# Expert results re-laid by DMA and two transposes taken off TensorE, in a planned two-layer transformer kernel

## The chip, the cores and the metric

The kernel runs on one core of one Trainium2 chip. The metric is device time in microseconds (us): the median of several executions, each counted from start to end on the device. A profile is one further execution, recorded instruction by instruction.

## What is computed

The input x is 8 batches of 256 tokens with 128 channels, in fp32. Six residual blocks follow one another, cut here to what matters:

```python
x = x + 0.5 * soft_moe(layernorm(x))          # L0_ffn: 16 experts, 64 slots each
x = x + linear_attention(layernorm(x))        # L0_attn: 16 heads of 8
x = x + 0.5 * soft_moe(layernorm(x))
x = x + 0.5 * ternary_glu(layernorm(x))       # L1_ffn: 128 -> 512 -> 512 -> 512 -> 128
x = x + favor_attention(layernorm(x))         # L1_attn: FAVOR+, 32 features a head
x = x + 0.5 * ternary_glu(layernorm(x))

# soft_moe, per expert e (slots = dispatch-weighted sums of tokens, for every batch):
gate = gelu(slots @ Wg[e] + bg[e]); up = slots @ Wu[e] + bu[e]
eout = (gate * up) @ Wd[e] + bd[e]            # "second product": 256 -> 128
y = combine @ eout                            # over all 16 * 64 slots

# linear attention, last steps:            out = heads(q @ kv) / norm;  out @ Wproj.T + bproj
# FAVOR+: KV = phiK.T @ V, Ksum = sum(phiK);   (phiQ @ KV) / (phiQ @ Ksum);  @ Wo.T + bo
```

## The kernel before, in words

**Order.** The work is not issued in program order. Each piece is a step with the engines it may run on, an assumed cost in ns, the buffers it reads and writes, and a key. `Plan.place` (line 123) simulates five queues (PE, ACT, DVE, POOL, SP) with these costs and with the delays of `LAG`, picks at each point the step that can start first, and so fixes the order of every engine's instructions and the buffer slots. `SHIFTS` (line 16) moves the keys of parts of the program against each other; it changes the order only, not the work. Where the plan expects PE to idle for long, `idle` (line 1397) puts in products with the identity that nobody reads.

**Two groups.** Batches 0 to 3 and 4 to 7 are two groups (`group`, line 1366). The second has keys 45 us later, so that one group's TensorE-heavy stage can run beside the other group's stages of DVE, ACT and POOL. In each group: twice `dispatch` for four batches, then `experts` (16 experts for the four batches together, two 64-slot halves per 128 rows), then `combine` per batch; after the first of the two, `linear` per batch. Then `glu` for pairs of batches, `favor` per batch, and `glu` again.

**Dispatch** (594). The normalized y of a batch, 128 partitions with 2 x 128 values each, is needed in four copies with 32 tokens to each row block. `replicated` (573) writes y to DRAM with four DMAs of 32 partitions (`spill`, line 579) and reads it back four times with 32 partitions of 4 KB (`spread`, line 586). The gathering product (line 691) uses TensorE as four tiles of 32 rows.

**Experts** (749). For expert e, `fetch` loads the weights We (384 KB, line 764) and, at even e, the biases bd of two experts by a broadcast (line 767). There are four buffers for them. `front` makes the hidden layer with full-array products (line 787), Gelu on ACT (793) and the product of gate and up on DVE (798). `back` makes the second product for a pair of experts at once (line 818). Its stationary operand has 64 columns, one batch's slots, so TensorE works as two tiles of 128 rows x 64 columns, and the two experts' results come out in the two halves of the partitions, as `combine` (line 859) wants them. DVE adds the bias and writes into the slots buffer (830). `back` of a pair is called after the front of the expert that follows the pair.

**Transposes.** There are two ways. `flip` (line 375) is a TensorE transpose through the identity, followed by a copy out of PSUM (`evacuated`, 382 and 384). `squares_turned` (440) transposes 32x32 squares on DVE (446), writes the tile to DRAM with one DMA (449) and reads it back with four DMAs that put the squares in place (455). The second way is used for the normalized inputs of `linear`, `glu` and `favor` and for FAVOR+'s query features. The first is used, among others, in `project` (888), for linear attention's output ahead of the product with Wproj (907), and in `favor` for the 2 x 128 columns of sums (`turn_sums`).

**Products in fp32** show as two matmul instructions each in the trace; a transpose shows as one.

All DMAs are issued from SP's queue, in order. A DMA that has to wait holds back all that stand behind it.

Of the kernel before, what the change touches and what calls it, by code (L numbers as in the profile page):

```python
# [9 lines left out]
F32 = mybir.dt.float32  # L10
AF = mybir.ActivationFunctionType
ALU = mybir.AluOpType
AX = mybir.AxisListType
P = 128

SHIFTS = (
    -2751, -1692, -1691, -12195, -784, -1588, -17523, -441, -1660, -895, -929, -659, -543, -591,
    -517, -633, -219, -357, -610, -370, -144, -340, -138, -261, -103, -124, -149, -112, -87,
    328, -365, -173, -179, -134, 14, 40, -32, 136, -182, -43, -162, -672, 13, -20, 26, 13, -393,
    -13, -49, 76, 108, 25, -337, -106, -98, -405, -124, -14, 106, -15, -91, -232, -26, -141, 72,  # L20
    179, -149, -60, -56, -94, -291, -910, -397, 168, -109, -149, -2, -601, -150, 12, -21, -762,
    -20, -100, 231, -63, -522, -971, -639, -490, -1134, 34, -143, -240, -1126, 30, 98, 272,
    -229, -245, 48, 535, -647, -666, -418, 7, 144, -282, -73, 220, 168, 36, -1118, -353, -720,
    -886, -200, -34, 24, 100, 11, -24, 70, 30, -50, -121, 47, 25, 9, -51, 143, -939, -125, -300,
    -662, -491, -371, -203, -437, -21, -285, -479, -125, 412, 243, 49, 284, 369, 566, -147,
    -339, 157, 267, -173, -269, 162, -518, -492, 53, 116, -414, -523, -222, -451, -400, -304,
    -82, 145, -77, -134, -36, -467, -865, -141, -372, -407, -524, -134, 12, 58, -154, 246, 41,
    -111, 22, 62, -756, -131, 38, -435, -1331, -683, -948, -2046, -2339, -2000, -3450, -2514,
    -3516, -3317, -2307, -1684,
)  # L30


# [184 lines left out]
def macaron_kernel(ctx: ExitStack, tc: tile.TileContext, i: dict, out: bass.AP):  # L217
# [10 lines left out]
    nc = tc.nc  # L228
    B, N, D = out.shape
    TT = N // P  # L230
# [126 lines left out]
    def ps_(*shape):  # L357
        return Buf("ps", (P, *shape))
# [4 lines left out]
    def dve(n, extra=0):  # L363
        return 58 + 1.07 * n + extra
# [4 lines left out]
    def flips(n):  # L369
        return 109.5 * n  # L370
# [3 lines left out]
    def flip(po, src):  # L374
        nc.tensor.transpose(po, src, ident)  # L375
# [64 lines left out]
    def squares_turned(z, n, cells, dst, out):  # L440


        flat = lambda: z()
        there = dram.tile([P, n // 32, 32], F32, tag=f"t{len(turns)}", name=f"t{len(turns)}")
        turns.append(there)
        step({"DVE": 58 + 1.07 * n}, lambda _: nc.vector.transpose(z(), z()), cells, cells)

        def spill(_):
            nc.sync.dma_start(there.rearrange("p k j -> p (k j)"), z())


        def place(_):
            squares = there.rearrange("(a i) (t f) j -> f i t a j", a=4, f=4)
            for f in range(4):
                nc.sync.dma_start(
                    dst()[32 * f : 32 * f + 32].rearrange("p (t a j) -> p t a j", a=4, j=32),
                    squares[f],
                )

        step({"SP": 475}, spill, cells, [there.name], lag=1.5 * n)  # L460
        step({"SP": 2000}, place, [there.name], out, lag=2.5 * n)

    turns = []

# [103 lines left out]


    dram = ctx.enter_context(tc.tile_pool(name="dram", bufs=1, space=bass.MemoryType.DRAM))  # L570
    spilled = [dram.tile([32, N // 32, D], F32, tag=f"y{b}", name=f"y{b}") for b in range(B)]

    def replicated(y, b):

        yr = Buf("k4", (P, N // 32, D))

        def spill(_):
            for k in range(4):
                nc.sync.dma_start(
                    spilled[b].rearrange("i (t k) d -> i k t d", k=4)[:, k],  # L580
                    y.ap[32 * k : 32 * k + 32],
                )

        def spread(_):
            for a in range(4):
                nc.sync.dma_start(yr.ap[32 * a : 32 * a + 32], spilled[b])

        step({"SP": 2500}, spill, [(y, t) for t in range(TT)], [("y", b)], lag=-1500)
        step({"SP": 1765}, spread, [("y", b)], [yr], lag=900)
        return yr  # L590


# [1 line left out]
    def dispatch(b, sl):  # L594
# [92 lines left out]
        def gathered(_):  # L687
            for c in range(N // 32):
                for a, po in enumerate(pos):
                    rows = slice(32 * a, 32 * a + 32)  # L690
                    mm(  # L691
                        po.ap, yr.ap[rows, c, :], ex.ap[rows, :, 32 * c : 32 * c + 32],
                        start=(c == 0), stop=(c == N // 32 - 1), tile_position=(32 * a, 0),
                    )

# [52 lines left out]

    def experts(sl):
        def whole(j):  # L750
            return [(sl, j, q) for q in range(BG)]

        filled = [(sl, "in", q, a) for q in range(BG) for a in range(4)]

        def eo():
            return sl.ap.rearrange("p j k b s -> p j (k b s)").rearrange(
                "p j (b n) -> p j b n", n=2 * S1
            )

        def fetch(e):  # L760
            we = Buf("we", (P, 6 * P + D))

            def run(_):
                nc.sync.dma_start(we.ap[:, 0 : 6 * P], i["We"][e])
                if e % 2 == 0:
                    for k in range(2):
                        nc.sync.dma_start(
                            we.ap[S * k : S * k + S, 6 * P :],
                            i["bd"][e + k].partition_broadcast(S),
                        )  # L770

            step(
                {"SP": 475 if e % 2 else 1400}, run, [(sl, "in", BG - 2, 0)], [we],
                lag=1900 if e % 2 else 1000,
            )
            return we

        def front(e, we):
# [28 lines left out]
                step({"DVE": dve(256, 59)}, up, [pe, ga], [(ht, c)])  # L807
            return ht

        def back(j, wes, hts):  # L810

            po = ps_(BG, P)

            def down(_):
                for q in range(BG):
                    for c in range(2):
                        for k in range(2):
                            mm(  # L818
                                po.ap[S * k : S * k + S, q, :], hts[k].ap[:, c, ts(q, S)],
                                wes[k].ap[:, ts(4 + c, P)], start=(c == 0), stop=(c == 1),  # L820
                                tile_position=(0, S * k),
                            )

            step(
                {"PE": 1880}, down,
                [*wes, *((ht, c) for ht in hts for c in range(2))], [po],
            )

            def biased(_):
                nc.vector.tensor_tensor(  # L830
                    eo()[:, j, :, 0:D], po.ap,
                    wes[0].ap[:, 6 * P :].unsqueeze(1).to_broadcast([P, BG, D]), ALU.add,
                )

            step({"DVE": dve(512)}, biased, [wes[0], po], whole(j))

            def twos(_):
                nc.gpsimd.memset(eo()[:, j, :, D : D + 1], 2.0)

            step({"POOL": 65}, twos, [], whole(j))  # L840

        got = []
        for e in range(E):
            plan.part()
            we = fetch(e)
            got.append((we, front(e, we)))
            if e % 2 == 0 and e:
                back(e // 2 - 1, *zip(*got[e - 2 : e]))
        back(NJ - 1, *zip(*got[E - 2 :]))
        return eo  # L850

    def combine(b, comb, sl, eo):
# [3 lines left out]
        for t in range(TT):  # L856
            def gather(_, t=t):
                for j in range(NJ):
                    mm(  # L859
                        po.ap[:, t, 0 : D + 1], comb.ap[:, j, ts(t, P)], eo()[:, j, q, 0 : D + 1],  # L860
                        start=(j == 0), stop=(j == NJ - 1),
                    )

            step(
                {"PE": mms(*[D + 1] * NJ)}, gather,
                [(comb, u) for u in range(4)] + [(sl, j, q) for j in range(NJ)], [(po, t)],
            )
        rc = Buf("sm", (P, TT))

# [17 lines left out]

    def project(b, oh, w):

        pt = ps_(TT, P)  # L890
        ot = Buf("k1", (P, N))

        def turn(_):
            for t in range(TT):
                flip(pt.ap[:, t, :], oh.ap[:, t, :])

        step({"PE": flips(TT)}, turn, [oh], [pt], takes=[ot])
        evacuated(lambda: ot.ap, lambda: pt.ap.rearrange("p t c -> p (t c)"), [pt], [ot], N)
        projected_onto(b, ot, w)

    def projected_onto(b, ot, w):
# [291 lines left out]
    def favor(b):  # L1193
# [103 lines left out]
            [(phi, 0, c) for c in range(4)],  # L1297
            lambda: qk.ap.rearrange("p a b n -> p (a b n)"), [(qk, t) for t in range(TT)],
        )
        pk, pkt = ps_(2, P), ps_(2, P)  # L1300
        kvm = Buf("k1", (P, 2, P))

        def sums(_):
# [13 lines left out]
                m4of.unsqueeze(1).unsqueeze(3).to_broadcast([P, 2, 4, M]), ALU.mult,  # L1317
            )

        def turn_sums(_):  # L1320
            for m in range(2):
                flip(pkt.ap[:, m, :], kvm.ap[:, m, :])

        step(
            {"PE": 1020}, sums, [*((phi, 1, c) for c in range(4)), v1], [pk], takes=[kv, kvm]
        )
        step({"DVE": 340}, blocks, [pk], [kvm])
        step({"PE": flips(2)}, turn_sums, [kvm], [pkt])
        evacuated(
            lambda: kv.ap, lambda: pkt.ap.rearrange("p a (c n) -> p a c n", c=4), [pkt], [kv], N  # L1330
        )


# [148 lines left out]
```

## Time and profile before

| | before |
|---|---|
| median of 3 runs | 740.42 us (740.34 to 740.69) |
| the profiled execution | 743.85 us |
| its span, first to last instruction | 742.1 us |
| granted TensorE clock | 0.998 |
| TensorE (PE) busy | 728.8 us, 98% |
| DVE / ACT / POOL busy | 517.2 / 410.7 / 306.1 us |
| packets of the kernel's DMA queue, share of 16 engines | 30.6% |

The profiled execution has 1.75 us outside its span and is 3.4 us longer than the median. PE is busy when any matmul is in flight; matmuls overlap, so the "mean ns of one" of a matmul is longer than the distance between two of them. PEld is the load of the stationary operand. SPq is SP's queue, which issues the DMAs. In the rows of groups, the columns are line, engine, operation, written<-read tiles, shape and count, then busy us and mean ns of one, then idle time ahead.

### The profile page before, as it was taken

The numbers are of one execution on the slowest core, as the hardware profiler recorded it, in microseconds if no ns is written. First come the engines' busy times: TensorE is split into PE (matmuls) and PEld (weight loads), VectorE is DVE, ScalarE is ACT, GpSimd is POOL, SyncE is SP. The second block draws the span as 40 slices with busy tenths as digits, with TensorE's granted clock in tenths as the row PEclk, the third lists the DMA queues.
The fourth block names the chain that finished last, engine by engine and source line by source line (L and its number), as shares of the span: only waits on it lengthen the run. The fifth ranks groups of instructions, "written<-read, shape, count | busy, mean of one in ns | idle before, by whom it ended". The sixth has DMA issues, their size and how long they took to land.

```text
span 742.1 us, 15296 instructions
## 1 busy us (share of the span) xinstructions
PE 728.8 (98%) x5814; PEld 609.5 (82%) x5814; DVE 517.2 (70%) x1103; ACT 410.7 (55%) x774; POOL 306.1 (41%) x419
## 2 busy tenths in 40 slices
PE   8999999998999999999999999999999999999998
PEld 7878888997889988889878879788687677878787
DVE  6999965577868798975564274455998978855442
ACT  4889967257665577884553240433555664363331
POOL 7989446133427752459910022000745545211000
PEclk9999999999999999999999999999999999999999
DMA  5553432333330526333631210200344244120100
GB/s 143 150 140 118 139 93 94 109 81 97 126 114 2 146 83 197 99 94 119 171 99 52 85 29 1 57 0 15 78 114 95 42 118 81 32 60 14 42 1 29
DMA packets 102105, 62.34 MB, mean 84 GB/s; under 512 B 73104, under 2 KB 88848, under 8 KB 102032
## 3 DMA queue, kind: packets, MB, share of 16 engines
q1 hardware_dynamic: 102032, 61.36, 30.6%
q8 instruction: 46, 0.75, 0.4%
q14 instruction: 27, 0.22, 0.1%
HBM read 49.80 MB, written 11.53 MB: 83 GB/s over the span
## 4 chain that ended last, share of the span: by engine, by line
PE 87%; DVE 5%; DMA 3%; SPq 2%; issue 1%; POOL 1%; ACT 1%; POOLq 0%
PE ps L1077 27%; PE ps L787 14%; PE ps L818 8%; PE ps L859 8%; PE ps L691 6%; PE ps L615 4%; PE ps L1177 4%; PE ps L1147 4%; PE ps L1150 4%; PE ps L375 2%; DMA we<-in_We 1%; PE ps L1256 1%; DVE k L632 1%; PE ps L1307 1%; PE ps L1341 1%; PE ps L907 1%
## 5 line engine op out<-in xcount | busy, mean ns | idle before, releaser
L787 PE MATMUL ps<-slots,we 128*128 128x256 f32 x512 | 121.8, 384 | 4.0 <-DMA we<-in_We 2.3
L787 PEld LDWEIGHTS ps<-slots,we 128*128 128x128 f32 x512 | 94.7, 191 | 20.1 <-issue 5.2
L1077 PE MATMUL ps<-comb,slots 128*128 128x256 f32 x448 | 103.1, 381 | 0.0
L1077 PE MATMUL ps<-comb,comb 128*128 128x256 f32 x448 | 102.5, 381 | 0.0
L1077 PEld LDWEIGHTS ps<-comb,slots 128*128 128x128 f32 x448 | 83.6, 190 | 15.4 <-issue 3.9
L1077 PEld LDWEIGHTS ps<-comb,comb 128*128 128x128 f32 x448 | 83.6, 190 | 13.6 <-issue 2.5
L737 POOL TENSOR_TENSOR comb<-comb,k 128x1024 f32<-128x1024 f32 x32 | 75.1, 2369 | 33.5 <-DVE k L384 14.0
L793 ACT ACTIVATE k<-ps,small 128x256 f32<-128x256 f32 x128 | 56.5, 475 | 48.4 <-PE ps L787 46.1
L382 ACT COPY k<-ps 128x512 f32<-128x512 f32 (+2 forms) x55 | 28.5, 519 | 93.8 <-PE ps L1077 83.1
L670 POOL TENSOR_TENSOR comb<-comb,sm 128x1024 f32<-128x1024 f32 x32 | 60.9, 1911 | 41.4 <-DVE sm L665 41.4
L798 DVE SCALAR_TENSOR_TENSOR k<-ps,small,k 128x256 f32<-128x256 f32 x128 | 57.2, 475 | 29.2 <-ACT k L793 28.5
L412 POOL TENSOR_SCALAR sm<-sm 128x2 f32<-128x2 f32 x52 | 10.0, 193 | 153.1 <-DVE sm L406 140.1
L657 ACT ACTIVATE comb<-comb,sm 128x256 f32<-128x256 f32 x128 | 63.3, 497 | 13.7 <-PE ps L691 7.4
L1091 DVE TENSOR_TENSOR comb<-ps,k 128x512 f32<-128x512 f32 x48 | 32.9, 687 | 49.0 <-PE ps L1077 25.5
L818 PEld LDWEIGHTS ps<-we,k 128*64 128x64 f32 x1024 | 55.3, 137 | 9.2 <-issue 4.7
L615 PE MATMUL ps<-k,seT 128*128 128x256 f32 x256 | 61.7, 383 | 0.8 <-DVE k L495 0.5
L818 PE MATMUL ps<-we,k 128*64 128x128 f32 x1024 | 62.2, 275 | 0.0
L691 PE MATMUL ps<-comb,k 32*128 32x256 f32 x1024 | 59.9, 380 | 0.1
L859 PEld LDWEIGHTS ps<-slots,comb 128*128 128x128 f32 x512 | 58.4, 192 | 1.5 <-issue 1.3
L859 PE MATMUL ps<-slots,comb 128*128 128x129 f32 x512 | 59.6, 276 | 0.0
L1099 ACT ACTIVATE comb<-comb 128x512 f32<-128x512 f32 x48 | 30.0, 629 | 51.0 <-DVE comb L1091 50.8
L691 PEld LDWEIGHTS ps<-comb,k 32*128 32x128 f32 x1024 | 51.4, 185 | 5.6 <-issue 1.4
(144 smaller groups left out, 1303.7 us busy)
## 6 DMA issues: line engine op xcount, KB each, us to landing
we<-in_We SPq DMA_DIRECT2D x64, 384.0 KB, 3.8
k<-y SPq DMA_DIRECT2D x64, 128.0 KB, 2.9
t<-comb SPq DMA_DIRECT2D x8, 512.0 KB, 2.8
k<-t SPq DMA_DIRECT2D x32, 128.0 KB, 3.5
y<-k SPq DMA_DIRECT2D x64, 32.0 KB, 1.9
we<-in_bd SPq DMA_DIRECT2D x64, 32.0 KB, 3.6
t<-k SPq DMA_DIRECT2D x16, 128.0 KB, 1.7
k<-t SPq DMA_DIRECT2D x64, 32.0 KB, 2.3
```

The lines of the kernel that those rows point to most:

```text
L615: mm(pl.ap[:, j, :], seT[:, 2 * u + j].rearrange("p k s -> p (k s)"), yt.ap, start=True, stop=True,)
L657: nc.scalar.activation(ex.ap[:, 4 * h + j, :], comb.ap[:, 4 * h + j, :], AF.Exp, bias=mx.ap[:, j : j + 1], accum_out=mx.ap[:, 4 + j : 5 + j],)
L670: nc.gpsimd.tensor_tensor(ex.ap[:, part], ex.ap[:, part], mx.ap[:, 8:12].unsqueeze(2).to_broadcast([P, 4, N]), ALU.mult,)
L691: mm(po.ap, yr.ap[rows, c, :], ex.ap[rows, :, 32 * c : 32 * c + 32], start=(c == 0), stop=(c == N // 32 - 1), tile_position=(32 * a, 0),)
L737: nc.gpsimd.tensor_tensor(raw, raw, mb.ap.unsqueeze(1).to_broadcast([P, 4, N]), ALU.subtract)
L787: mm(pe.ap[:, m, :], we.ap[:, ts(2 * m + c, P)], sl.ap[:, j, k, :, 0:S], start=True, stop=True,)
L793: nc.scalar.activation(ga.ap, pe.ap[:, 0, :], AF.Gelu, bias=bg[:, e, c : c + 1])
L798: nc.vector.scalar_tensor_tensor(ht.ap[:, c, :], pe.ap[:, 1, :], bu[:, e, c : c + 1], ga.ap, ALU.add, ALU.mult,)
L818: mm(po.ap[S * k : S * k + S, q, :], hts[k].ap[:, c, ts(q, S)], wes[k].ap[:, ts(4 + c, P)], start=(c == 0), stop=(c == 1), tile_position=( ...
L859: mm(po.ap[:, t, 0 : D + 1], comb.ap[:, j, ts(t, P)], eo()[:, j, q, 0 : D + 1], start=(j == 0), stop=(j == NJ - 1),)
L1077: mm(bank.ap[:, o], w(k)[:, c, ts(o, P)], rhs().rearrange("p (c n) -> p c n", c=2)[:, c, :], start=(start and o + c == 0), stop=(stop and ...
L1091: nc.vector.tensor_tensor(C(i, k)(), bank.ap.rearrange("p o n -> p (o n)"), other(), ALU.add)
```

## The change

Four things change in the work.

- `replicated`: y goes to DRAM with one DMA of 128 partitions. The four reads fetch 32 x 4 pieces of 1 KB each in place of 32 of 4 KB, and the gathering product picks its columns by another index.
- `experts`: the second product is made for one expert at a time, right after the next expert's front, with full-array products: the stationary operand holds 128 slots, of two batches. The result is added to the bias in a buffer `moved` of 128 x 2 x 128, and two DMAs move its halves into the slots buffer. The bias comes with We from the host, already broadcast (448 KB a fetch), and the DMAs for bd are gone.
- `project`: the transpose of linear attention's output goes by `squares_turned`.
- `favor`: the transpose of the sums goes by `squares_turned`.

The planner's assumed costs of the DMA steps are others, and all of `SHIFTS` is replaced. The diff, with the numbers of `SHIFTS` and the host's lines cut:

```diff
 SHIFTS = (
-    -2751, -1692, -1691, -12195, -784, -1588, -17523, -441, -1660, -895, -929, -659, -543, -591,
...
+    -2645, -927, -925, -41, -149, -109, -109, -110, -145, -159, -38, -195, -225, 8, 143, -82,
...
 )
...
-        step({"SP": 475}, spill, cells, [there.name], lag=1.5 * n)
-        step({"SP": 2000}, place, [there.name], out, lag=2.5 * n)
+        step({"SP": 335}, spill, cells, [there.name], lag=1.1 * n - 850)
+        step({"SP": 2400 + 0.7 * n}, place, [there.name], out, lag=1.2 * n - 300)
...
-    spilled = [dram.tile([32, N // 32, D], F32, tag=f"y{b}", name=f"y{b}") for b in range(B)]
+    spilled = [dram.tile([P, N], F32, tag=f"y{b}", name=f"y{b}") for b in range(B)]
...
         def spill(_):
-            for k in range(4):
+            nc.sync.dma_start(spilled[b], y.ap.rearrange("p t d -> p (t d)"))
+
+        def spread(_):
+            blocks = spilled[b].rearrange("(k i) n -> i k n", k=4)
+            for a in range(4):
                 nc.sync.dma_start(
-                    spilled[b].rearrange("i (t k) d -> i k t d", k=4)[:, k],
-                    y.ap[32 * k : 32 * k + 32],
-                )
-
-        def spread(_):
-            for a in range(4):
-                nc.sync.dma_start(yr.ap[32 * a : 32 * a + 32], spilled[b])
-
-        step({"SP": 2500}, spill, [(y, t) for t in range(TT)], [("y", b)], lag=-1500)
-        step({"SP": 1765}, spread, [("y", b)], [yr], lag=900)
+                    yr.ap[32 * a : 32 * a + 32].rearrange("i (k t) d -> i k (t d)", t=TT), blocks
+                )
+
+        step({"SP": 335}, spill, [(y, t) for t in range(TT)], [("y", b)], lag=-500)
+        step({"SP": 1830}, spread, [("y", b)], [yr], lag=900)
         return yr
...
-                        po.ap, yr.ap[rows, c, :], ex.ap[rows, :, 32 * c : 32 * c + 32],
+                        po.ap, yr.ap[rows, TT * (c % 4) + c // 4, :], ex.ap[rows, :, 32 * c : 32 * c + 32],
...
             def run(_):
-                nc.sync.dma_start(we.ap[:, 0 : 6 * P], i["We"][e])
-                if e % 2 == 0:
-                    for k in range(2):
-                        nc.sync.dma_start(
-                            we.ap[S * k : S * k + S, 6 * P :],
-                            i["bd"][e + k].partition_broadcast(S),
-                        )
...
+                nc.sync.dma_start(we.ap, i["We"][e])
+
+            step({"SP": 475}, run, [(sl, "in", BG - 2, 0)], [we], lag=1500)
             return we
...
-        def back(j, wes, hts):
-
-            po = ps_(BG, P)
+        def back(e, we, ht):
+
+
+            j, k = e // 2, e % 2
+            po = ps_(NB, P)
+            moved = Buf("k1", (P, NB, P))
 
             def down(_):
-                for q in range(BG):
+                for r in range(NB):
                     for c in range(2):
-                        for k in range(2):
-                            mm(
-                                po.ap[S * k : S * k + S, q, :], hts[k].ap[:, c, ts(q, S)],
-                                wes[k].ap[:, ts(4 + c, P)], start=(c == 0), stop=(c == 1),
-                                tile_position=(0, S * k),
-                            )
...
+                        mm(
+                            po.ap[:, r, :], ht.ap[:, c, ts(r, P)], we.ap[:, ts(4 + c, P)],
+                            start=(c == 0), stop=(c == 1),
+                        )
 
             def biased(_):
                 nc.vector.tensor_tensor(
-                    eo()[:, j, :, 0:D], po.ap,
-                    wes[0].ap[:, 6 * P :].unsqueeze(1).to_broadcast([P, BG, D]), ALU.add,
-                )
...
+                    moved.ap, po.ap, we.ap[:, 6 * P :].unsqueeze(1).to_broadcast([P, NB, P]),
+                    ALU.add,
+                )
+
+            def place(_):
+                for h in range(2):
+                    nc.sync.dma_start(
+                        eo()[S * k : S * k + S, j, h::2, 0:D], moved.ap[S * h : S * h + S]
+                    )
...
+            step({"PE": mms(*[P] * 4)}, down, [we, (ht, 0), (ht, 1)], [po], takes=[moved])
+            step({"DVE": dve(256)}, biased, [we, po], [moved])
+            step({"SP": 1340}, place, [moved], cells, lag=-300)
...
-            if e % 2 == 0 and e:
-                back(e // 2 - 1, *zip(*got[e - 2 : e]))
-        back(NJ - 1, *zip(*got[E - 2 :]))
+            if e:
+                back(e - 1, *got[e - 1])
+        back(E - 1, *got[E - 1])
         return eo
...
     def project(b, oh, w):
 
-        pt = ps_(TT, P)
         ot = Buf("k1", (P, N))
-
-        def turn(_):
-            for t in range(TT):
-                flip(pt.ap[:, t, :], oh.ap[:, t, :])
-
-        step({"PE": flips(TT)}, turn, [oh], [pt], takes=[ot])
-        evacuated(lambda: ot.ap, lambda: pt.ap.rearrange("p t c -> p (t c)"), [pt], [ot], N)
+        squares_turned(
+            lambda: oh.ap.rearrange("p t d -> p (t d)"), N, [oh], lambda: ot.ap, [ot]
+        )
         projected_onto(b, ot, w)
...
-        step({"PE": flips(2)}, turn_sums, [kvm], [pkt])
-        evacuated(
-            lambda: kv.ap, lambda: pkt.ap.rearrange("p a (c n) -> p a c n", c=4), [pkt], [kv], N
+        squares_turned(
+            lambda: kvm.ap.rearrange("p a n -> p (a n)"), N, [kvm],
+            lambda: kv.ap.rearrange("p a c n -> p (a c n)"), [kv],
         )
```

## The prediction, made before the result was known

> **What bounds the kernel now.** I read the page first: the engines' busy shares, and the chain that ended last.
>
> ```profile
> PE 728.8 (98%) x5814; PEld 609.5 (82%) x5814; DVE 517.2 (70%) x1103; ACT 410.7 (55%) x774; POOL 306.1 (41%) x419
> PE 87%; DVE 5%; DMA 3%; SPq 2%; issue 1%; POOL 1%; ACT 1%; POOLq 0%
> ```
>
> TensorE is the bound from end to end: a change gains what it takes out of PE, and loses what it makes PE wait. Next, how much PE waits (columns: us in total, times, longest us):
>
> ```profile
> PE ps L787 <- DMA we<-in_We: 2.3, 2, 2.2
> PE ps L1399 <- POOL ident masks.py:199: 1.6, 1, 1.6
> PE ps L787 <- ACT comb L657: 1.2, 1, 1.2
> PE ps L375 <- DVE k L708: 1.1, 1, 1.1
> ```
>
> All such waits together are 8.9 us, so a better order alone can't win more than that. The costliest groups give the work that the change touches:
>
> ```profile
> L818 PE MATMUL ps<-we,k 128*64 128x128 f32 x1024 | 62.2, 275 | 0.0
> L859 PE MATMUL ps<-slots,comb 128*128 128x129 f32 x512 | 59.6, 276 | 0.0
> L375 PE MATMUL ps<-ident,k 128*128 128x128 f32 x112 | 23.5, 288 | 3.2 <-DVE k L708 1.1 <-POOL k L420 0.7 <-DVE k L1000 0.5
> ```
>
> A busy PE isn't a PE at its peak, so I went to PE's timeline, where the distance between the starts of two rows is what a block really takes. Around the last second product:
>
> ```profile
> 438.72 3.62 PE L1077 MATMUL ps<-comb,slots 128*128 128x256 f32 x16
> 442.26 1.97 PE L818 MATMUL ps<-we,k 128*64 128x128 f32 x32
> 444.16 1.99 PE L1077 MATMUL ps<-comb,slots 128*128 128x256 f32 x8
> 445.99 1.28 PE L859 MATMUL ps<-slots,comb 128*128 128x129 f32 x10
> ```
>
> and around a block of two pairs:
>
> ```profile
> 221.04 3.71 PE L818 MATMUL ps<-we,k 128*64 128x128 f32 x64
> 224.68 0.43 PE L375 MATMUL ps<-ident,sm 128*128 128x128 f32 x2
> ```
>
> One pair takes 442.26 to 444.16, 1.90 us, two take 3.64, so a pair in full flow takes 1.74 (54.5 ns an instruction) and 0.16 is paid on entry. The neighbours pay too. Full-array 256-column instructions follow each other every 216 ns (eight in 1.73 us in the chain). The x16 ahead takes 3.54 where 16 x 0.216 is 3.46 (+0.08), the x8 behind takes 1.83 (+0.10). So one excursion into 128x64 tiles costs 0.16 + 0.08 + 0.10 = 0.34 us, with no wait shown. Between full-array blocks nothing is paid: the eight L787 just ahead (436.99 to 438.72) take the plain 1.73.
>
> **The second product.** Removed: 1024 instructions at 54.5 ns, 55.8 us. Added: 64 experts x 8 = 512 full-array instructions. The nearest row is L859's (128 stationary columns, 129 moving): the chain has 32 of them in 3.57 us, 111.6 ns each, so 57.1 us. In full flow that is 1.3 us worse. The switches: the timeline has 28 blocks of L818. Twenty stand between full-array blocks and save 0.34 each, 6.8. Eight stand beside a block in 32-row or 32-column tiles, which pays a switch anyway; there I take the entry alone, 0.16, so 1.3. Sum: 1.3 - 6.8 - 1.3 = **-6.8 us** on PE. The Trainium skill, TensorEngine Tiling (Array Packing), section "Theoretical Speedup", speaks against the change: a stationary side of up to 64 columns gains up to 2x from packing. By that rule alone, with the 128 columns filled by two batches' slots, the two forms tie; by the rows' full-flow rates the change loses 1.3. The same page's "Key Properties" says that a change of tiling mode drains the array, with no price. The rows put 0.34 us on it, 28 times, and I take the rows.
>
> Beside PE: 64 DVE adds of 128x256 from PSUM (413 ns, L911) for 32 of 128x512 (688 ns), +4.4 us on an engine at 70%. SP issues 128 more DMAs of 32 KB (0.59 us each by y<-k, 75.5 us) and 64 fewer bd (0.59 us, -37.8). The add waits for `down` as before. The two DMAs wait for the add, and behind them in SP's queue stand We fetches and the other group's spills: about 0.41 + 1.2 us for each. That hits little, since a fetch has to wait for the buffer that the same `down` frees. SP's waits show it (L764 behind L818: 112.4 us in 18 waits). The pairwise `back` frees two of four buffers at once, one front (1.73 us) before the next weights are wanted; 3.8 us to landing doesn't fit, and PE's 2.3 us wait on We is the remnant. Freed one by one, the lead is two experts, 2 x (1.73 + 0.90) = 5.3 us, against about 6 (1.6 of hold, 4.4 for 448 KB in proportion): closer, not ample. Ends 0 and -2.3; I take **-1**.
>
> What is late next is `combine`: at the end of each of four expert blocks the last result comes after 0.41 + 1.2 + about 1.9 us to landing, 3.5 in place of 0.69. Cover at the last block was one L1077 product (444.16 to 445.99), and more of these stand ready; the earlier blocks have the other group's work. Ends 0 and 4 x 2.8 = 11.2; the nearest row has cover, so **+1**.
>
> **The two turns.** Removed: 16 times two transposes at 109 ns, 32 x 0.109 = **-3.5 us** on PE, and 16 copies out of PSUM (0.37 to 0.41 us). Added: 16 DVE transposes (0.44, L446), and on SP 16 x (0.33 + 4 x 0.61) = 44 us:
>
> ```profile
> k<-y SPq DMA_DIRECT2D x64, 128.0 KB, 2.9
> y<-k SPq DMA_DIRECT2D x64, 32.0 KB, 1.9
> ...
> t<-k SPq DMA_DIRECT2D x16, 128.0 KB, 1.7
> k<-t SPq DMA_DIRECT2D x64, 32.0 KB, 2.3
> ```
>
> The delay grows: 0.44 + 0.33 + 1.7 + 2.45 + 2.3 = 7.2 us (the same turn of linear's input ran from 141.32 to 150.43, 9.1 us), for 1.09 from flip to L907 (167.34 to 168.43). So +6.1 to +8.0 us a turn. FAVOR+'s eight lie among L1077 products of another pair: nothing. Linear's eight lie between `combine` and the next `dispatch`; only the last batch of each group delays the experts, so two exposures, up to 2 x 6.1 = 12.2 us. Between 160 and 170 us PE alternates linear's pieces with L787 of the other group: cover exists, though small waits at 175.8, 269.5, 272.1 and 291.6 us say that it isn't ample. Ends 0 and 12.2; **+2**.
>
> **One spill of y.** SP saves 4 x 0.59 - 0.33 = 2.0 us on each of 16 dispatches (the 0.33 is t<-k, the same 128 x 1 KB). The reads get four times the pieces: by 0.42 (k<-y) and 0.61 (k<-t, smaller pieces yet) I take +0.1 us each, 0.4 a dispatch. This is behind PE except in the first 56 us, where the chain, in order of time, runs through eight such issues:
>
> ```profile
> 43.72 0.55 SPq L579
> ...
> 48.11 0.04 issue
> 48.16 2.57 DMA y<-k
> 50.73 0.01 issue
> 50.74 1.93 DVE k L708
> ```
>
> Two spills in place of eight DMAs take 0.66 for 4.4 us there. But DVE is busy 49.8 of those 56 us and will be the next bound. Ends 0 and -3.8; **-1.5**, a little over PE's 1.1 us wait behind L708.
>
> **Order.** The new assumed costs are nearer to the rows (a placement 2579 ns for 4 x 0.61; it was 2000). Nothing of its own: 0, within the 8.9 us of waits either way.
>
> **Sum:** -6.8 - 1 + 1 - 3.5 + 2 - 1.5 = -9.8 us. The profiled execution's span goes from 742.1 to 732.3 (743.85 to about 734 with what lies around it). The median lies 3.4 us below that execution, so I take the same difference from it: 740.42 - 9.8 = 730.6.
>
> **Rivals.** (a) All added waits find cover, and the start and the We waits give their full ends: -6.8 - 3.5 - 3.8 - 2.3 = -16.4, 724.0. For it: PE's long list of ready products after 380 us. Against: DVE in the first 56 us. (b) PE loses its 10.3 us, but hops and turns lay half of it bare (+5.5) and nothing else comes: 735.6. For it: the small waits at 160 to 292 us. (c) Slower: SP's queue at the layer change. Each group's four linear turns add 4 x 2.77 = 11 us of issues where four input turns and four spreads already stand, and the hops of the other group's experts wait among them; a placement that waits for its spill holds the We fetches, L787 starves, and the cover goes with it. It decides once over 5.2 us is bare at each of the two changes; at 7 us each, 740.4 - 10.3 + 14 = 744. For it: SP's in-order queue, 112 us of fetch waits. Against: the spills give back 2.0 us per dispatch at that very place. (d) The change doesn't do what it says: the 0.16 us on entry belongs to stationary operands that are loaded late and not to the tiles, so 64 single blocks pay it too. Then the second product costs +1.3 - 8.1 + 64 x 0.16 = +3.4, the turns give back 3.5, the rest is +0.5: 740.8. Against: the neighbours' 0.08 and 0.10, and full-array blocks side by side that pay nothing.
>
> **How the numbers follow.** Chances: the sum 0.56 (730.6, from 726 to 735), (a) 0.12, (b) 0.17, (c) 0.10, (d) 0.05. A measurement can tell 0.2% (1.5 us) from no change. Faster: the sum, (a) and (b), 0.85; same: (d), 0.05; slower: (c), 0.10. The range takes in (a) and (b) and stops short of (d) and (c): 723.5 to 739.
>
> **What would show it.** Right: the second product in 512 full-array instructions at 112 ns, its neighbours at plain rates, PE busy down by about 10 us, transposes x80 for x112, PE's wait list still under 10 us. Wrong: PE waits on slots<-k or k<-t DMAs, L787 behind We for over 3 us, or idle products (L1399's) in the middle of the run.

## The result: 1.1% slower, and the profile after

| | before | changed |
|---|---|---|
| median (range) | 740.51 us (740.34 to 740.69) | 748.88 us (746.72 to 751.30) |
| ratio to before, 95% interval | | 1.0114 (1.0078 to 1.0150) |
| profiled execution / its span | 743.85 / 742.1 us | 747.5 / 745.8 us |
| PE waits, sum of the list | 8.9 us | 20.9 us |
| span less these waits | 733.2 us | 724.9 us |
| time of SP's DMA issues, summed over the trace | 249 us in 457 | 315 us in 553 |

The forecast was 730.6. The two profiled executions differ by 3.7 us and the medians by 8.4: what lies between a profiled execution and the median (3.4 us before) did not carry over. The changed kernel's executions spread over 4.6 us, these four of before over 0.35; but 55 later ones of the kernel before spread over 5.0 (738.3 to 743.3), so the narrow range says little.

A part of those 3.4 us can be seen in the profile of before. Behind its longest wait on We (2.2 us, over at 182.3) the granted TensorE clock is 0.50 from 183.0 to 186.4 us. A windows view of the stretch (length, busy us and instructions of PE, PEld, DVE, ACT, POOL, then clock, DMA share, GB/s) reads

```profile
180.00:190.00 10.00, 7.83 (x36) 6.73 (x36) 6.22 (x17) 4.82 (x10) 2.70 (x3) 0.83 0.47 117
```

so some 1.7 us of clock are lost there (10 x 0.17, an estimate); with the wait that is 3.9 us. The execution was a rare one: of 92 later executions of the kernel before, 90 show a clock of 0.999 or 1.000 over the whole span, and the two at 0.998, like this one, took 742.9 and 743.3 us. The changed kernel's profiled execution shows 1.000; its slowest, of 751.3 us, 0.995.

Busy shares, and the chain that ended last, from the changed kernel's page:

```profile
PE 721.0 (97%) x5262; PEld 609.0 (82%) x5262; DVE 518.3 (69%) x1133; ACT 421.1 (56%) x784; POOL 312.1 (42%) x421
PE 72%; DMA 13%; SPq 7%; DVE 4%; issue 2%; POOL 1%; ACT 1%; DVEq 0%; POOLq 0%; ACTq 0%
```

PE is busy 7.8 us less, as it was meant to be, though some of that is the clock of before. But the chain is no longer PE's: DMA and SP's queue hold 20% of it, for 5% before. What PE waits for in the changed kernel (total, times, longest, us; L897 is the product after linear attention's turn, L777 the experts' first, L918 linear's first, L1195 and L1327 FAVOR+'s):

```profile
PE ps L897 <- DMA k<-t: 7.9, 5, 3.0
PE ps L777 <- DMA we<-in_We: 4.4, 7, 1.4
PE ps L918 <- DMA k<-t: 2.2, 2, 1.9
PE ps L1385 <- POOL ident masks.py:199: 1.6, 1, 1.6
PE ps L1195 <- DMA k<-t: 1.5, 2, 1.3
PE ps L1327 <- DMA kv<-t: 1.5, 2, 1.2
```

The longest, in the chain of the changed kernel (start us, us, what):

```profile
201.99 4.11 DMA t<-k
206.11 0.02 issue
206.12 0.61 SPq L454
...
208.04 0.04 issue
208.09 2.26 DMA k<-t
210.35 0.14 issue
210.48 0.68 PE ps L897 x4
```

A turn's spill is in flight for 4.11 us, where the median is 2.0. It was issued right behind two hops and a We load, as SP's timeline shows:

```profile
200.01 1.25 SPq L823 DMA_DIRECT2D slots<-k  x2
201.36 0.54 SPq L763 DMA_DIRECT2D we<-in_We  x1
201.99 0.39 SPq L448 DMA_DIRECT2D t<-k  x1
206.12 2.58 SPq L454 DMA_DIRECT2D k<-t  x4
```

PE works in order: the L777 products behind L897 wait with it, and show no wait of their own.

```profile
210.48 0.68 PE L897 MATMUL ps<-WprojT,k 128*128 128x128 f32 x4 [2.99 <-DMA k<-t]
211.00 1.03 PE L777 MATMUL ps<-slots,we 128*128 128x256 f32 x4
```

Most of the loss is in one stage: of the 12.0 us by which the listed waits grew, 9.7 lie between 160 and 310 us. The windows view of that stage, of the kernel before:

```profile
160.00:310.00 150.00, 146.15 (x1235) 128.03 (x1235) 123.93 (x289) 103.46 (x219) 73.37 (x105) 0.99 0.36 102
```

and of the changed kernel:

```profile
160.00:310.00 150.00, 137.16 (x1084) 122.61 (x1084) 115.64 (x281) 91.94 (x198) 63.51 (x95) 1.00 0.51 142
```

PE is busy 9.0 us less in these 150 us, and the DMA engines' share rises from 0.36 to 0.51. The issues and landings of the changed kernel:

```profile
we<-in_We SPq DMA_DIRECT2D x64, 448.0 KB, 4.2
k<-y SPq DMA_DIRECT2D x64, 128.0 KB, 2.8
slots<-k SPq DMA_DIRECT2D x128, 64.0 KB, 2.5
t<-k SPq DMA_DIRECT2D x32, 128.0 KB, 2.0
```

A hop (slots<-k: one of the two DMAs that move an expert's result into the slots buffer) is 64 KB. The prediction had 32.

### The profile page after: what moved, and what is told of

It is laid out like the page before. It is cut to its first block, busy times and chain, and to the rows that moved or that the text cites. A ratio compares the mean times of both kernels' runs of the same rounds, so it can differ in the third digit from the quotient of the medians.

```text
span 745.8 us, 14551 instructions
## 1 busy us (share of the span) xinstructions
PE 721.0 (97%) x5262; PEld 609.0 (82%) x5262; DVE 518.3 (69%) x1133; ACT 421.1 (56%) x784; POOL 312.1 (42%) x421
## 4 chain that ended last, share of the span: by engine, by line
PE 72%; DMA 13%; SPq 7%; DVE 4%; issue 2%; POOL 1%; ACT 1%; DVEq 0%; POOLq 0%; ACTq 0%
PE ps L1067 21%; PE ps L777 11%; PE ps L854 7%; PE ps L690 6%; PE ps L810 6%; PE ps L614 5%; SPq L454 5%; DMA we<-in_We 4%; DMA t<-k 3%; PE ps L1137 3%; PE ps L1140 3%; DMA k<-t 3%; PE ps L1167 3%; PE ps L374 1%; PE ps L1327 1%
## 5 line engine op out<-in xcount | busy, mean ns | idle before, releaser
L777 PE MATMUL ps<-slots,we 128*128 128x256 f32 x512 | 121.7, 382 | 4.6 <-DMA we<-in_We 4.4
L777 PEld LDWEIGHTS ps<-slots,we 128*128 128x128 f32 x512 | 93.1, 190 | 20.8 <-issue 6.1
L381 ACT COPY k<-ps 128x512 f32<-128x512 f32 (+2 forms) x50 | 25.4, 507 | 72.7 <-PE ps L1067 58.8
L810 PEld LDWEIGHTS ps<-we,k 128*128 128x128 f32 x512 | 63.9, 192 | 2.7 <-issue 0.6
L810 PE MATMUL ps<-we,k 128*128 128x128 f32 x512 | 65.7, 275 | 0.0
L411 POOL TENSOR_SCALAR sm<-sm 128x2 f32<-128x2 f32 x52 | 10.3, 199 | 109.1 <-DVE sm L405 106.4
```

The lines of the kernel that those rows point to most:

```text
L777: mm(pe.ap[:, m, :], we.ap[:, ts(2 * m + c, P)], sl.ap[:, j, k, :, 0:S], start=True, stop=True,)
L810: mm(po.ap[:, r, :], ht.ap[:, c, ts(r, P)], we.ap[:, ts(4 + c, P)], start=(c == 0), stop=(c == 1),)
```

## The experiments

Theories: **W**, the turns' own delay; **S**, the hops crowd SP's queue (S1) and the DMA engines (S2), and what else comes by DMA is late; **O**, the new order is poor by itself. In e1 to e7 the changed kernel's order is kept instruction by instruction. The interval of the changed kernel is 2.7 us to either side, so a difference from it is known to about 3 us.

**e1 and e2: nobody waits for the turns.**

```diff
-                mm(po.ap[:, t, :], ot.ap[:, ts(t, P)], w, start=True, stop=True)
+                mm(po.ap[:, t, :], ident if free else ot.ap[:, ts(t, P)], w, start=True, stop=True)
```

and in e2 FAVOR+'s `kv.ap[:, m, c, :]` becomes `ones32` as well.

> The changed kernel in its own order, but linear attention's output product reads the identity in place of the turned array: the turn's DVE transpose and its five DMAs a batch are still issued, and TensorE waits for none of them (the output leaves attention's result out). Theory W (TensorE's in-order queue reaches that product before the turned array has landed, 7.9 us of waits in the changed kernel's profile): 739 to 741 us, 8 to 10 under the changed kernel. Theory S (the experts' hops crowd SP's queue and the DMA engines and make all that comes by DMA late): at most 3 us faster, 746 or more, with the waits moving to the expert weights. Theory O (the new order is poor by itself): 746 or more.

> As the run before it, and FAVOR+'s product over the sums reads a constant of ones as well, so neither of the two new turns is waited for (the sums are left out of the result). W: another 1.5 to 2.5 us under the run before it, about 737 to 739, since the changed profile shows 1.9 us of TensorE waits on that turn. S and O: no change against the run before it beyond 1 us.

e1: 742.44 us, ratio 1.0042 (1.0027 to 1.0056), 6.4 under the changed kernel and between what W and S had asked for. e2: 742.75, 1.0038 (1.0026 to 1.0049), no better. In e2, PE's wait list has more on We (4.4 us in the changed kernel):

```profile
PE ps L777 <- DMA we<-in_We: 7.3, 8, 1.4
```

With nothing to wait for at either turn the kernel is still 0.4%, some 3 us, slower than before. The turn is where most of the loss shows, not all that makes it: W is half right at best.

**e3: no hops.** The add writes into the slots buffer, and `place` issues nothing.

```diff
-                    moved.ap, po.ap, we.ap[:, 6 * P :].unsqueeze(1).to_broadcast([P, NB, P]),
+                    eo()[:, j, 2 * k : 2 * k + 2, 0:D], po.ap,
+                    we.ap[:, 6 * P :].unsqueeze(1).to_broadcast([P, NB, P]),
```

> The changed kernel in its own order, but the DVE add writes its result straight into the slots buffer, in the wrong rows, and the 128 DMAs of the hops are gone (expert results are mixed between slots). W: linear's turn is still waited for, with somewhat shorter landings: 743 to 747. S: SP loses 76 us of issues and all waits behind them; spills and weights land in time, 738 to 741. O: 746 or more.

730.80 us, 0.9874 (0.9858 to 0.9890): 18.1 us under the changed kernel, more than any theory asked for. PE's longest waits in e3:

```profile
PE ps L894 <- DMA k<-t: 2.1, 3, 1.1
PE ps L1382 <- POOL ident masks.py:199: 1.6, 1, 1.6
PE ps L915 <- DMA k<-t: 0.5, 1, 0.5
```

and e3's window from 160 to 310 us:

```profile
160.00:310.00 150.00, 147.35 (x1155) 133.48 (x1155) 124.83 (x302) 102.08 (x218) 70.89 (x101) 1.00 0.44 127
```

The same turns, in the same places, are waited for 2.1 us in place of 7.9, and no wait on We is listed; PE is busy 147.4 us of that window. The spill shown above stands in e3's queue, too, behind the same eight reads of y, and there its reads begin 2.3 us after it, not 4.1:

```profile
196.67 0.34 SPq L448 DMA_DIRECT2D t<-k  x1
198.96 2.53 SPq L454 DMA_DIRECT2D k<-t  x4
```

Over the turns' spills from 150 to 310 us (L448, issue to landing) the median is 2.8 us and the longest 4.8 in the changed kernel, 2.1 and 3.8 in e3, 1.7 and 2.0 before. This is S, and against O in this order: without hops the order gives what the PE sum promised.

**e4: the old spill of y**, in the changed order (`replicated` and the gathering product's index as before).

> The changed kernel in its own order with y written and read back as before (four DMAs of 32 partitions, four reads of 4 KB pieces): SP issues 48 DMAs more, 33 us. All theories: slower than the changed kernel. W: by 1 to 3 us, in the first 60 us and where SP is dense between 160 and 300 us. S: by 4 us or more, since SP's queue is what decides. If it is not slower, the one spill is worth nothing in this order.

763.27 us, 1.0315 (1.0275 to 1.0355), 14.4 us slower than the changed kernel. SP's issues rise from 315 to 344 us. The head of PE's wait list in e4:

```profile
PE ps L777 <- DMA we<-in_We: 13.3, 8, 4.3
PE ps L897 <- DMA k<-t: 9.3, 6, 3.3
```

So 29 us more of issues in SP's queue cost 14. The profiled executions differ by 12.4 us and show how: the listed waits come to 29.0 us for 20.9, and behind three waits of 2.7 to 4.3 us the clock falls. One of these stretches of e4:

```profile
220.00:230.00 10.00, 8.66 (x46) 7.69 (x46) 6.29 (x16) 3.77 (x7) 5.72 (x8) 0.83 0.21 47
```

Between 222.4 and 225.7 us it is 0.50 there, and a block of eight L810 takes 1.71 us from start to start (223.09 to 224.80), for the 0.89 of the changed kernel. Three times 1.7 us of lost clock and 8.1 of waits make 13.2. The four executions of e4 show clocks of 0.984 to 0.993. So a long wait can be paid twice, though not every one is: the changed kernel's 2.99 us has no such stretch behind it. The one spill is worth much more in this order than the 1.5 us that I gave it; the order was planned for it.

**e5 and e6: what of a hop costs.** e5 keeps every hop's issue and its wait for the add, and moves 4 KB (64 x 64 bytes) of the 64; it writes only where `combine` reads for two batches of four; e6 moves all of it, from a constant, so that SP doesn't wait for the add.

```diff
-                        eo()[S * k : S * k + S, j, h::2, 0:D], moved.ap[S * h : S * h + S]
+                        eo()[S * k : S * k + S, j, h, 0:16], eo()[S * h : S * h + S, j, 2 * k, 64:80],
```

```diff
-                        eo()[S * k : S * k + S, j, h::2, 0:D], moved.ap[S * h : S * h + S]
+                        eo()[S * k : S * k + S, j, h::2, 0:D], ident[S * h : S * h + S].unsqueeze(1).to_broadcast([S, NB, P]),
```

> The changed kernel in its own order; the DVE add writes into the slots buffer in the wrong rows, and each of the 128 hop DMAs still waits for it and is still waited for, but moves 64 pieces of 64 bytes (4 KB) in place of 128 pieces of 512 bytes (expert results are mixed between slots). Theory S1 (what costs is SP's in-order queue: the issue of 128 DMAs, their waits, and all that stands behind them): 744 to 748, near the changed kernel. Theory S2 (what costs is the transfers, on the 16 DMA engines that the weights and spills share): 731 to 735, near the run without hops.

> The changed kernel in its own order with all 128 hop DMAs in full size, but they read a constant, so that SP doesn't wait for the add of the expert (expert results are left out); SP still waits until the rows that they overwrite have been read. Theory S1a (the wait for the add holds SP's queue, up to 52 us of waits ahead of these DMAs in the changed profile): 734 to 739. Theory S1b (the issue time alone, 128 times 0.6 us in a dense queue): 744 to 748. Theory S2: 744 to 748 as well, with SP's waits at this line much shorter.

e5: 738.48 us, 0.9977 (0.9967 to 0.9988). e6: 744.31, 1.0047 (1.0034 to 1.0060). So of e3's 18.1 us, 748.9 - 738.5 = 10.4 go with the bytes, and 738.5 - 730.8 = 7.7 with issues and waits. The wait for the add is worth 748.9 - 744.3 = 4.6. All but the 7.7 carry the 3 us of the changed kernel, so which of the two parts is larger isn't shown; and fewer bytes also shorten SP's own work (its issues sum to 298 us in e5, for 315). Neither S1 nor S2 alone; e5 landed between its two answers.

**e7: DVE makes the hop**, in the changed order: two adds of 64 partitions in `biased`, each written to the rows where it belongs (the edit is e10's). In that order an add can write slots that the pair's second expert has yet to read; this run computes something else there, unlike what its expectation says.

> The changed kernel in its own order, computing all of it: the hop is made by DVE, which adds the bias in two halves of 64 partitions and writes each to the rows where it belongs, so there are no hop DMAs and no buffer between. DVE does 128 adds of 64 x 256 elements in place of 64 of 128 x 256 (about 0.41 us each, 26 us more of DVE, busy 69% now). If the hops are the loss: 731 to 737, faster than both kernels. If DVE becomes late in the expert stage: 738 to 744.

741.73 us, 1.0015 (1.0006 to 1.0024). PE's wait for We falls to 0.2 us, but the adds' 27.6 us more on DVE show: PE waits for DVE 5.9 us in seven rows of its list. 10.9 us over e3, which leaves the hop out without DVE's part.

**e8 to e11: parts of the change, planned anew.** The planner's order doesn't survive an edit, so SHIFTS was searched again for each, on the planner's own span.

```diff
+                    rows = slice(S * h, S * h + S)
+                    nc.vector.tensor_tensor(
+                        eo()[S * k : S * k + S, j, h::2, 0:D], po.ap[rows],
+                        we.ap[rows, 6 * P :].unsqueeze(1).to_broadcast([S, NB, P]), ALU.add,
+                    )
...
+            step({"DVE": 2 * dve(256)}, biased, [we, po], cells)
```

> The whole-array second product with its hops and the one spill of y, but both turns by TensorE as before; the numbers of SHIFTS searched anew for this mix, on the planner's own span (718.8 us there; before 721.8, the changed kernel 714.5). SP's issues fall by 44 us against the changed kernel. Theory S (hops and turns together overfill SP's queue and the DMA engines; either alone is bearable): 735 to 742. Theory H (the hops alone are the loss, the more so in the expert stage, where the turns don't stand): 744 to 750.

> The two turns through DRAM and the one spill of y, with the second product as before (pairs of 64-column tiles, biases by their own DMAs); SHIFTS searched anew (721.7 us on the planner's span). TensorE loses 3.5 us against before, the tile switches stay. Theory S: 737 to 741. Theory W (the turns' waits are a loss by themselves, hops or not): 743 or more.

> Everything of the changed kernel but the hops, which DVE makes by two adds of 64 partitions each, planned as such, with the slots written only after they have been read; SHIFTS searched anew (718.8 us on the planner's span). Theory S and H: SP has what the run without hops had, so 730 to 737, faster than both kernels, unless DVE's 27 us more show. If 740 or more, the gain of the run without hops belonged to the work left out and not to SP and the DMA engines.

> As the run before it, with both turns by TensorE again; SHIFTS searched anew (721.8 us on the planner's span). The turns' worth once SP is free of the hops: S says 2 to 4 us slower than the run before it (733 to 741); W says faster than it by 2 or more.

| | plan | measured | ratio (95%) | behind plan |
|---|---|---|---|---|
| e8 product with hops, one spill | 718.8 | 749.48 | 1.0122 (1.0092 to 1.0151) | 30.7 |
| e9 turns, one spill | 721.7 | 753.25 | 1.0160 (1.0136 to 1.0185) | 31.5 |
| e10 adds, turns, one spill | 718.8 | 747.62 | 1.0092 (1.0069 to 1.0114) | 28.8 |
| e11 adds, one spill | 721.8 | 748.99 | 1.0116 (1.0091 to 1.0141) | 27.2 |

All missed their S windows; e8 fell where the hops alone were to be the loss (H), e9 where the turns were (W). e10 and e11 have no hops and still don't beat before, so e3's 730.8 can't be claimed for any mix without hops; by e10's expectation, 740 or more even gives e3's gain to the work left out. DVE's two adds take 2 x 0.42 us where the plan has 0.66, 64 times, 11.5 us more than planned; how much of it PE pays is not shown. e9 says that the turns with the one spill lose by themselves in a new order. But each of the four has another order, so a control was due.

**e12 to e15: the same search for both works**, unaltered but for SHIFTS.

> The kernel before with all of its work unaltered; SHIFTS searched anew from zeros on the planner's span (727.3 us there, where the numbers of before give 721.8). Theory S (the work decides): 740.4 + 5.5 = 744 to 748, the planner's difference and no more. Theory O (an order searched on the planner's span alone falls further behind its plan than the order of before does, whatever the work): 752 or more.

> As the run before it from another seed of the search (727.7 us on the planner's span). S: 744 to 748. O: 752 or more. The two together show how far two such orders differ.

> The changed kernel with all of its work unaltered; SHIFTS searched anew from zeros in the same way (725.8 us on the planner's span). S: it falls behind its plan by the 34 us of the changed kernel or more, 758 to 766, over both orders of the kernel before. O: 30 us behind its plan like every new order, 752 to 758, level with the new orders of the kernel before.

> As the run before it from another seed of the search (719.3 us on the planner's span). S: 752 to 760. O: 746 to 751, under the new orders of the kernel before by what the planner says (8 us).

| | plan | measured | ratio (95%) | behind plan |
|---|---|---|---|---|
| before | 721.8 | 740.5 | 1 | 18.7 |
| e12 before, order a | 727.3 | 746.21 | 1.0075 (1.0054 to 1.0096) | 18.9 |
| e13 before, order b | 727.7 | 747.63 | 1.0100 (1.0079 to 1.0120) | 19.9 |
| changed | 714.5 | 748.88 | 1.0114 (1.0078 to 1.0150) | 34.4 |
| e14 changed, order a | 725.8 | 758.31 | 1.0240 (1.0211 to 1.0269) | 32.5 |
| e15 changed, order b | 719.3 | 758.33 | 1.0246 (1.0223 to 1.0270) | 39.0 |

O falls as the whole cause. A new order costs the work of before 6 to 7 us, so it may also be why e10 lost much of e3's gain; but at equal search the changed work is still 11 us slower. The work of before lies 19 us behind each of these plans; part of that is the tile switches, which the plan doesn't price. The changed work lies 32 to 39 behind. The head of PE's wait list in e12:

```profile
PE ps L786 <- DMA we<-in_We: 1.7, 2, 1.5
PE ps L1398 <- POOL ident masks.py:199: 1.6, 1, 1.6
PE ps L614 <- DVE sm L664: 1.5, 1, 1.5
```

and in e15:

```profile
PE ps L777 <- DMA we<-in_We: 9.5, 7, 4.3
PE ps L918 <- DMA k<-t: 7.1, 7, 1.8
PE ps L897 <- DMA k<-t: 2.5, 3, 1.0
```

In e15 the waits on DMAs come to 20.5 us, for 17.9 in the changed kernel, and fall on other lines: which wait ends last is the order's choice, that DMAs end last is the work's.

**e16 to e18: the hops in another order, and orders searched with late DMAs.** e16 is e15 with e3's edit.

> The changed kernel in the second of its newly searched orders (758.3 us), with the hops taken out as before: the add writes into the slots buffer in the wrong rows (expert results are mixed between slots). If the hops are the main price in any order: 738 to 744, 14 to 20 us less. If the 18 us were a matter of the changed kernel's own order: 750 or more.

> The changed kernel with all of its work unaltered; SHIFTS searched on a replay of the planned order in which every DMA lands late by a random amount (0.5 us on the average) and a change of TensorE's tiles costs 0.18 us each way (714.1 us on the planner's own span, 730.8 on the replay). If trust in the delays is the cause: 735 to 742. If the DMAs overfill SP and the DMA engines, whatever the order: 745 or more.

> The kernel before with all of its work unaltered, SHIFTS searched in the same way (722.8 us on the planner's span, 744.7 on the replay). The control for the run before it: 736 to 744 in both theories; what it gains over the kernel before is owed to the search alone.

e16: 748.24 us, 1.0099 (1.0084 to 1.0114), 10.1 under e15. e17: 747.91, 1.0098 (1.0076 to 1.0121). e18: 741.91, 1.0012 (1.0002 to 1.0022). The hops' price holds in another order, but is 10 us there and not 18. That is nearly all of the 11 us at equal search: without hops the changed work only ties with the new orders of before (746 and 748), though its PE is busy 723.5 us for 729.5 and 730.3 there. What costs it those 6 to 7 us is open. Slack for late DMAs doesn't rescue the changed work: e17 is 6.0 us over e18. No version beat the kernel before and computed all of it.

## Why the prediction was wrong

**The second product, -6.8, and the turns' -3.5: right in kind.** Around a whole-array block the changed kernel's timeline reads

```profile
162.94 0.61 PE L962 MATMUL ps<-kv,k 128*128 128x129 f32 x4
163.39 1.06 PE L810 MATMUL ps<-we,k 128*128 128x128 f32 x8
164.28 0.66 PE L985 MATMUL ps<-kv,k 128*128 128x144 f32 x4
```

0.89 us from start to start, 8 x 111 ns, and nothing paid on either side. Span less listed waits fell by 8.3 us, for 10.3 forecast, and some 1.7 of the 8.3 are the lost clock in the profile of before; in e3 it is 11.0. Transposes are x80. Rival (d) is out.

**The hops, +1: the step that failed.** I priced them where they end, at `combine`, and there PE waits for none of them. Their price is on others: 18.1 us in this order (e3), 10.1 in another (e16). I had written that what they hold in SP's queue "hits little", because a We fetch waits for the same `down`. I had named the other group's spills behind them and given these nothing; the turns' and y's DMAs stand there, and e6 puts the wait for the add at 4.6 us. The bytes on the DMA engines I had not counted at all, with a hop of 64 KB taken for 32; they are worth some 10 (e5).

**The turns, +2.** Waits on landings of turns (k<-t, kv<-t, and 0.4 us on t<-k) went from 0.3 to 13.5 us, 9.8 of them at the two new turns and 3.7 at turns that were there before. The 7.2 us of delay took a spill at 1.7 us, as it landed before. In the stage where linear's turns stand the median is now 2.8 and the longest 4.8, and the order is fixed for one landing time. Without hops it is 2.1 and 3.8, so the turns' own DMAs have a part in this.

**We, -1:** 2.3 became 4.4 us. I had also read the 2.3 as a standing loss. Most of it is one wait of 2.2 us, in an execution whose clock few others share, so there was probably little there to win; no second trace of that kernel shows it. **y's spill, -1.5:** the experts begin at 57.4 us in place of 61.6, and undoing it costs 14.4 (e4): right in sign, and in this order far too small. **Order, 0 within 8.9 us:** that bound was for gains. On the loss side none holds; other orders of the same work cost before 6 to 7 us and the changed work 9.

**The sum** also carried over the 3.4 us between the profiled execution and the median. Between the profiled executions the forecast misses by 13.5 us, between the medians by 18.2; that step accounts for the other 4.7. That e3, at 730.8, lies beside the forecast of 730.6 is chance: the forecast has the hops in it.

Rival (c), SP's queue at the layer change, named the place and the wait, at 0.10 and 744. It also named the hops waiting among the turns' DMAs as the way. I held it low because the spills give back 2.0 us a dispatch there, and never summed the queue in that stage. From 150 to 200 us the issues take 73% of the time, and from 250 to 300 us 71% (before 47 and 65), each with its waits on top.

**Open:** why e8 to e11 and e16 lie 27 to 32 us behind their plans without hops or without turns. What they share is the one spill with its reads and the planner's shorter delays for DMA steps; neither was tried alone. e17 speaks against the delays as the only cause. In e10 the clock, at 0.992 to 0.995, makes up some 4.6 us of its 28.8 (an estimate).

## What to carry to other kernels

When work moves from the bound engine to DMAs, price the DMAs by what stands behind them in the issuing queue and beside them on the DMA engines, in the stage where they fall, and not by their own deadline or by a share of the whole span. In an order fixed beforehand each new landing is a place where the bound engine can stop with ready work behind it, so what counts is how late landings come in that stage, and not their median over the whole run. When a planner's order changes with every edit, compare works at equal search, and look for what can be taken out with the order kept.

## What the runs showed of the hardware

- A change of TensorE's tiles there and back cost about 0.34 us, paid partly by the full-array neighbours; two 128x64 tiles in full flow made a pair's product in 1.74 us, the whole array in 1.78.
- DVE added from one half of the partitions into the other (e10). 64 x 256 elements took 0.42 us, as long as 128 x 256 (0.42, L816): half the partitions, no time saved.
- With the issues and waits kept, the hops' bytes cost 10 us of the kernel (to about 3), though the DMA engines' mean share in that stage was 0.51.
- Behind some waits of PE (2.2 us before; 4.3, 3.4 and 2.7 in e4) the granted clock was 0.50 for 3.4 us, with PE busy again and its products at half their rate; behind others (3.0 us in the changed kernel) it stayed at 1.00.
